# Macaron block in float32: values ahead of the correction in the speculated units, and a ninth half of expert weights loaded early

## The chip, the cores and the metric

The kernel runs on one core of one Trainium2 chip. The metric is the device time of one execution in microseconds. A profile of one execution gives, for each engine, what it did and what it waited for: PE (TensorE; its weight loads are listed as PEld), DVE (VectorE), ACT (ScalarE), POOL (GpSimd) and SP (SyncE, which here only issues transfers). "Lnnn" is a line of the kernel.

## The reference

The input is 8 batches of 1024 tokens of width 512, all float32. Three residual steps follow each other: half of a mixture-of-experts layer, an attention, and half of the same mixture-of-experts layer again.

```python
x = x + 0.5 * ffn(layernorm(x))
x = x + attention(layernorm(x))
x = x + 0.5 * ffn(layernorm(x))

def ffn(x):                                # 32 experts, each takes 8 tokens of each batch
    probs = softmax(x @ gate_w.T + gate_b, axis=tokens)
    vals, idx = top_k(probs, 8)            # over the tokens, for each expert
    merged = sum_k vals * x[idx]           # one row for each expert and batch
    h = gelu([merged, 1] @ w1)             # w1: 32 x 513 x 2048
    o = [h, 1] @ w2                        # w2: 32 x 2049 x 512
    return scatter_add(zeros, idx, vals * o)

def attention(x):                          # 16 heads of 32, causal linear attention
    q, k, v = exp(x @ Wq.T + bq), exp(x @ Wk.T + bk), x @ Wv.T + bv
    num = q . cumsum(k v^T);  den = q . cumsum(k)
    return (num / den) @ Wo.T + bo
```

## The kernel before

**Stages.** First the gate of the first expert layer for all batches, then the first 32 experts (`experts(0, ...)`), then the attention batch by batch, then the experts again (`experts(1, ...)`) and a last pass that adds their outputs to the chosen tokens. The expert weights come from memory in halves of 2 MB (`load_half`), four for each expert: two of `w1`, two of `w2`. `place` gives the tile for half number n; eight tiles are used in turn. In the last experts these are tiles of the attention's own memory (`xt0` to `xt2`, `un0`, `un1`), two of a pool `big1`, and one, `c9`, in memory of the spilled units. `preload` loads halves 0 to 3 while the attention still runs.

**Attention.** A batch has 8 chunks of 128 tokens, numbered c, and 4 units of two chunks, numbered u. For batches 0 to 3 a unit's projections to q, k and v are made in the attention (`project`). For batches 4 to 7 (`NB0 = 4`) they were made from the input alone while the first experts waited for weights (`speculate`) and were spilled to memory in `ahead_d`. When the attention comes to such a unit (`project_rest`), the spilled values (`pre`, 1.5 MB for a unit) are read back and corrected for what the first expert layer added to x. `project_rest` is a generator with four steps:

1. scales: one over the deviation spread over the partitions (L641, L649), `pmr` on POOL (L651), `pre` scaled on POOL (L655), and the next unit's `pre` requested (L713)
2. the correction of q and k: matmuls L667 into the PSUM tiles `sp0` and `sp1`, sums on DVE (L676) into `un`, exponentials on ACT (L679)
3. the values: matmuls L687, sums on DVE (L697) into `va`
4. running sums of the keys on DVE (L720) and the product `qk` on POOL (L731)

A chunk then takes: `scores` (L777, into `sp0` and `sp1`; masked on DVE at L788 for one half, copied by ACT at L793 and masked by POOL at L795 for the other), at even c the `denominators` (L739, reciprocal at L747) and their spreading (L758, L765), `turn_keys` (L827, L829), `project_out` of the chunk before (L891, L898 and its moments), and `attend` (numerators L841 and L853, product with the denominators L862, key-value sums L873).

**Around a chunk.** `begin(b + 1)` scatters the first experts' outputs into the next batch's tokens (`scatter_two`, L293, L300, L308, with moments at L314). `route(b - 1)` is the gate of the second expert layer for the batch before: logits scaled (`gate_scale`), the 8 largest of each expert chosen (`choose`: top 8 at L408, their replacement at L413, their indices at L415, softmax at L417 and L420), the chosen weights transposed (L523), merged rows (L543), and their transposes (L566). All three are generators that the loop in `attention` advances with `next`, once or more in a chunk.

**What sets the order.** The order in the program is a scheduler's, which starts from the order in which the loop issues the steps and moves instructions of an engine's queue by its own estimates. On the chip each engine takes its queue in that order. PSUM tiles named `ps_...` mostly share one tag `mm` with three banks; `sp0` and `sp1` have one bank pair each and serve the scores, the correction and the spreading of denominators.

**The seam to the last experts.** After the attention, 32 indirect transfers (L1557, L1558) issued by POOL gather the chosen tokens and weights into `xg` and `pg`. `prepare`, called in the middle of the experts, turns `pg`. The experts' loop issues `first(e)` (w1, L1233) and `second(e - 1)` (w2, L1256) as their halves arrive.

Of the kernel before, what the change touches and what calls it, by code (L numbers as in the profile page):

```python
# [15 lines left out]
P = 128  # L16
# [4 lines left out]
def kernel(  # L21
# [382 lines left out]
    def choose(t, lg, rows, g, name, listed=False, el=None):  # L404


        top = t.p2.tile([P, 8], F32, tag="top", name=f"top_{name}")
        nc.vector.max(top[rows, :], lg[rows, :])  # L408
        pinned = el is not None
        sm = t.p2.tile([P, 3], F32, tag="sm", name=f"sm_{name}")  # L410
        nc.vector.tensor_scalar_mul(sm[rows, 0:1], top[rows, 0:1], -1.0)
        rest = pm[:, g, :]
        nc.vector.match_replace(rest[rows, :], top[rows, :], lg[rows, :], -1.0e30)  # L413
        if listed and not pinned:
            nc.vector.max_index(chosen_idx[rows, g, :], top[rows, :], lg[rows, :])  # L415
        el = el if pinned else lg
# [6 lines left out]
        if pinned:  # L423
            tc.keep_in_program_order(kept)
        nc.vector.reciprocal(sm[rows, 2:3], sm[rows, 1:2])
        if pinned:
            return rest, sm[rows, 2:3], top
        return rest, sm[rows, 2:3]
# [51 lines left out]
    def route(t, s, b, el=None):  # L480
# [28 lines left out]
        chosen, r, *top = choose(t, lg, rows, g, f"b{b}", True, el)  # L509
# [113 lines left out]
    def project_rest(t, s, b, u):  # L623
# [35 lines left out]

        qkT = open_unit(t, s, b, u)  # L660
# [21 lines left out]
        yield  # L682

        ps = [t.mm.tile([P, D], F32, tag="mm", name=f"ps_v_{b}_{u * U + i}") for i in range(U)]
        for i in range(U):
            r = slice(E * ((b + i) % 4), E * ((b + i) % 4 + 1))
            nc.tensor.matmul(  # L687
                ps[i],
                lhsT=pmr[r, i * P : (i + 1) * P],
                rhs=s["oWv", i][r, :],  # L690
                start=True,
                stop=True,
            )
        for i in range(U):
            c = u * U + i
            va = t.a2.tile([P, D], F32, tag="va", bufs=3, name=f"va_{b}_{c}")
            nc.vector.scalar_tensor_tensor(  # L697
                va,
                pre[:, (2 * NDC + i * 2) * UT : (2 * NDC + i * 2 + 2) * UT],
                rs[:, c : c + 1],  # L700
                ps[i],
                ALU.mult,
                ALU.add,
            )
            s["va", b, c] = va
# [244 lines left out]
    def attention(t, early, preload):  # L950
# [46 lines left out]
        last = None  # L997
        for b in range(B):
            for c in range(NCH):
# [23 lines left out]
                if b == B - 1 and c == NCH - 2:  # L1023
                    late.close()
                    preload(1)
                    preload(2)
                    preload(3)
                    el = end.enter_context(tc.tile_pool(name="el", bufs=1, side="right")).tile(
                        [P, S], F32, name="el"
                    )  # L1030
                    gate = route(t, s, b, el)
                if rest and c % U:
                    turn_keys(t, s, b, c)
                    next(ahead)
                    next(gate, None)
                scores(t, s, b, c)
# [28 lines left out]
                if last is not None:  # L1065
                    project_out(t, s, *last)
                    if c == 0:
                        for h in range(2):
                            store_x(out, s["xt", b - 1][0], b - 1, h)
                        gate_sums(t, s, b - 1, range(NCH // 2, NCH))  # L1070
                        gate = route(t, s, b - 1)
                    if c == NCH // 2:
                        gate_sums(t, s, b, range(c))
                    if b == B - 1 and c == NCH - 2:
                        gate_sums(t, s, b, range(NCH // 2, c))
                    if b == B - 1 and c == NCH // 2:
                        store_x(out, s["xt", b][0], b, 0)
                if c % U == 0:
                    spread_denominators(t, s, b, c // U)
                else:  # L1080
                    if rest and c > 1:
                        next(begun, None)
                    next(ahead, None)
# [5 lines left out]
                if rest and c % U == 0:  # L1089
                    next(ahead)  # L1090
# [101 lines left out]
    def experts(f, place, loaded, beside=iter(()), aside=None):  # L1192

        with ExitStack() as stack:
            hp = stack.enter_context(tc.tile_pool(name=f"hp{f}", bufs=2))
# [99 lines left out]
            for e in range(E + 2):  # L1295
# [12 lines left out]
                if e == E // 2 and aside is not None:  # L1308
                    aside()
# [212 lines left out]
    keep, loaded, pools = ExitStack(), {}, {}  # L1522

    def place(n, shape, name):
        k = n % 8
# [17 lines left out]
    with ExitStack() as stack:  # L1543
# [3 lines left out]
        tk = stack.enter_context(tc.tile_pool(name="tk", bufs=1))  # L1547
        out_rows = out.rearrange("b s d -> (b s) d")
        pmT_rows = pmT_d.rearrange("b s e -> (b s) e")


        xg = tk.tile([P, 2, K, D], F32, name="xg")
        pg = tk.tile([P, 2, K, E], F32, name="pg")
        for g in range(2):
            for k in range(K):
                at = bass.IndirectOffsetOnAxis(ap=chosen_idx[:, g, k : k + 1], axis=0)
                nc.gpsimd.indirect_dma_start(pg[:, g, k, :], None, pmT_rows, at)  # L1557
                nc.gpsimd.indirect_dma_start(xg[:, g, k, :], None, out_rows, at)  # L1558
        pgT = tk.tile([P, 2, K, E], F32, name="pgT")
        to = tk.tile([P, 2 * K], U32, name="to")  # L1560

        def prepare():


            for g in range(2):
# [103 lines left out]
```

## Time and profile before

| what | value |
| --- | --- |
| time, median of 3 runs | 2604.76 us (2601.95 to 2608.11) |
| the profiled execution's own time | 2606.22 us |
| its span, first to last instruction | 2604.5 us |
| mean granted TensorE clock | 0.915 |
| PE busy | 2190.8 us (84%) |
| DVE busy | 862.3 us (33%) |
| ACT busy | 500.4 us (19%) |
| POOL busy | 376.6 us (14%) |
| halves of expert weights | 256, of 2048 KB |

The span has four stages: the first gate to about 120 us, the first experts to about 812 us, the attention to about 1960 us, and the last experts to the end. In the profile's rows of 40 slices a digit is a share in tenths; a slice lasts 65.1 us. "PEclk" is the clock that TensorE was granted, as a share of full speed. In an answer by stretches of time, the columns after the stretch are its length, the busy time of each engine with the number of its instructions, the granted clock, the share of the time in which the 16 DMA engines were busy, and GB/s. In a timeline a row is a start, a duration, the engine, line and operation, what it writes and reads, a count, and in brackets how long the engine sat idle before it and whom it waited for.

### The profile page before, as it was taken

What the parts mean: (1) busy time and instruction counts of PE and PEld (TensorE: products, weight loads), DVE (VectorE), ACT (ScalarE), POOL (GpSimd) and SP (SyncE); (2) the same over time, 40 slices, a digit from 0 to 9 for tenths busy, and PEclk for the clock granted to TensorE, in tenths of its full rate; (3) what the DMA queues carried; (4) which work ended last, traced back from release to release, by engine and by line L of the source; (5) the groups of instructions that cost most, each with busy time, mean ns of one, the idle gap of its engine ahead of it and who ended that gap; (6) DMA issues with size and microseconds to landing.
All of it is one profiled execution on the core that took longest, in us unless ns stands there. A gap on an engine that the chain in (4) does not pass through costs nothing.

```text
span 2604.5 us, 41783 instructions
## 1 busy us (share of the span) xinstructions
PE 2190.8 (84%) x18679; PEld 1153.6 (44%) x18679; DVE 862.3 (33%) x1495; ACT 500.4 (19%) x965; POOL 376.6 (14%) x345
## 2 busy tenths in 40 slices
PE   8799999898986999999999989999986565555555
PEld 5354545444533666666666655555551111101111
DVE  6411111111102443444534466777750000100002
ACT  6310000000000322222223243343430000000000
POOL 0000000000000212111122145545324000000002
PEclk9999999999998999999999989989888878777788
DMA  7799999999996000010100233333159999999995
GB/s 276 305 426 427 427 427 427 426 427 428 427 429 255 1 18 1 21 50 20 52 9 19 79 110 124 106 113 109 68 210 389 425 427 428 428 428 428 428 427 239
DMA packets 95635, 668.22 MB, mean 257 GB/s; under 512 B 18254, under 2 KB 22606, under 8 KB 58592
## 3 DMA queue, kind: packets, MB, share of 16 engines
q1 hardware_dynamic: 73952, 621.71, 58.1%
q10 hardware_dynamic: 18432, 35.66, 3.5%
q0 software_dynamic: 3072, 8.19, 0.8%
q8 instruction: 146, 2.39, 0.4%
q14 instruction: 33, 0.27, 0.0%
HBM read 614.34 MB, written 48.23 MB: 254 GB/s over the span
## 4 chain that ended last, share of the span: by engine, by line
PE 50%; issue 23%; DMA 16%; DVE 5%; ACT 2%; POOL 1%; SPq 0%; POOLq 0%; ACTq 0%; DVEq 0%
DMA w<-in_w 11%; PE ps_o L891 8%; PE ps_k L603 4%; PE ps_q L603 4%; PE ps_v L811 4%; PE ps_sk L1143 3%; PE ps_sq L1143 3%; PE p_ps L1256 3%; PE h_ps L1233 3%; PE ps_n L841 2%; PE sp L777 2%; PE ps_n L853 2%; PE ps_sv L1160 2%; DMA xg<-out,chosen_idx 2%; PE ps_sc L293 1%
## 5 line engine op out<-in xcount | busy, mean ns | idle before, releaser
L1233 PE MATMUL h_ps<-w,mT 128*8 128x512 f32 x2048 | 294.4, 703 | 126.2 <-DMA w<-in_w 124.3
L1242 DVE STREAM_TRANSPOSE hs<-h_ps 128x512 f32<-128x512 f32 x64 | 45.9, 717 | 721.6 <-PE h_ps L1233 716.3
L1256 PE MATMUL p_ps<-w,pm 128*32 128x512 f32 x1024 | 168.9, 790 | 130.3 <-DMA w<-in_w 122.0
L891 PE MATMUL ps_o<-wo_sb,at 128*128 128x512 f32 x512 | 258.5, 652 | 0.2
L1233 PEld LDWEIGHTS h_ps<-w,mT 128*8 128x8 f32 x2048 | 51.2, 95 | 342.4 <-issue 208.7
L1256 PE MATMUL p_ps<-w,gl 128*32 128x512 f32 x1024 | 133.5, 654 | 38.6 <-DMA w<-in_w 38.3
L594 POOL TENSOR_TENSOR xt<-xt,bo_sb 128x512 f32<-128x512 f32 x32 | 45.8, 1447 | 763.1 <-PE ps_ocT L338 703.4
L1256 PEld LDWEIGHTS p_ps<-w,pm 128*32 128x32 f32 x1024 | 36.0, 127 | 265.7 <-issue 136.5
L891 PEld LDWEIGHTS ps_o<-wo_sb,at 128*128 128x128 f32 x512 | 102.0, 210 | 115.0 <-issue 110.0
L795 POOL TENSOR_SCALAR_AFFINE_SELECT am<-am 128x512 f32<-128x512 f32 x128 | 79.0, 642 | 398.7 <-ACT am L793 260.8
L314 DVE BATCH_NORM_STATS2 st<-xt 128x6 f32<-128x512 f32 x192 | 128.4, 684 | 5.1 <-DMA xt<-in_x 2.5
L603 PE MATMUL ps_k<-xnT,wk_sb 128*128 128x256 f32 x512 | 115.3, 383 | 10.8 <-ACT xnT L339 10.8
L1249 ACT ACTIVATE pm<-a 128x128 f32<-128x128 f32 x32 | 9.9, 309 | 586.5 <-DVE a L1244 580.5
L1143 PE MATMUL ps_sq<-xcT,wq_sb 128*128 128x256 f32 x512 | 118.7, 388 | 4.1 <-ACT xcT L241 4.1
L1143 PE MATMUL ps_sk<-xcT,wk_sb 128*128 128x256 f32 x512 | 117.4, 385 | 0.0
L1160 PE MATMUL ps_sv<-wv_sb,xcT 128*128 128x512 f32 x256 | 115.6, 599 | 0.0
L811 PE MATMUL ps_v<-wv_sb,xnT 128*128 128x512 f32 x256 | 115.1, 593 | 0.0
L603 PE MATMUL ps_q<-xnT,wq_sb 128*128 128x256 f32 x512 | 115.1, 382 | 0.0
L1143 PEld LDWEIGHTS ps_sq<-xcT,wq_sb 128*128 128x128 f32 x512 | 96.8, 193 | 35.3 <-issue 17.4
L1143 PEld LDWEIGHTS ps_sk<-xcT,wk_sb 128*128 128x128 f32 x512 | 96.8, 192 | 27.6 <-issue 15.0
L603 PEld LDWEIGHTS ps_k<-xnT,wk_sb 128*128 128x128 f32 x512 | 95.8, 190 | 28.6 <-ACT xnT L339 14.7
L777 PE MATMUL sp<-un 32*128 32x128 f32 x2048 | 104.8, 302 | 3.9 <-DVE un L676 3.8
(246 smaller groups left out, 2846.3 us busy)
## 6 DMA issues: line engine op xcount, KB each, us to landing
w<-in_w SPq DMA_DIRECT2D x256, 2048.0 KB, 29.8
xt<-in_x SPq DMA_DIRECT2D x31, 1024.0 KB, 10.8
pre<-ahead_d SPq DMA_DIRECT2D x16, 1536.0 KB, 6.5
ahead_d<-ahead_qk ACTq DMA_DIRECT2D x16, 1024.0 KB, 11.5
out<-xt SPq DMA_DIRECT2D x16, 1024.0 KB, 5.4
xs<-in_x ACTq DMA_DIRECT2D x16, 512.0 KB, 19.7
ahead_d<-ahead_v ACTq DMA_DIRECT2D x16, 512.0 KB, 11.0
pm<-pm SPq DMA_DIRECT2D x16, 128.0 KB, 2.5
```

What stands on the lines that cost most here:

```text
L314: nc.vector.bn_stats(st, xt[:, c, :])
L603: nc.tensor.matmul(ps[:, o, :], lhsT=w_sb[n][:, dc, oc * P : (oc + 1) * P], rhs=xnT[:, dc, :], start=(dc == 0), stop=(dc == NDC - 1),)
L777: nc.tensor.matmul(sp[r // 2][:, r % 2, og, :], lhsT=kT[hr, og, cols], rhs=qT[hr, og, cols], start=True, stop=True,)
L795: nc.gpsimd.affine_select(out=am[1][:, i, :, :], in_=am[1][:, i, :, :], pattern=[[0, NDC], [1, P]], compare_op=ALU.is_ge, fill=0.0, base=0 ...
L811: nc.tensor.matmul(ps, lhsT=s["xnT", b, c // U][:, dc, cols], rhs=w_sb["v"][:, dc, :], start=(dc == 0), stop=(dc == NDC - 1),)
L841: nc.tensor.matmul(ps[hr, og, :], lhsT=va[:, (og * HG + r) * HD : (og * HG + r + 1) * HD], rhs=am[r // 2][:, r % 2, og, :], start=(og == 0 ...
L853: nc.tensor.matmul(ps[hr, og, :], lhsT=kv[hr, og, :], rhs=qT[hr, og, cols], start=False, stop=True, skip_group_check=True,)
L891: nc.tensor.matmul(ps, lhsT=at[:, oc, :], rhs=w_sb["o"][:, oc, :], start=(oc == 0), stop=(oc == NDC - 1),)
L1143: nc.tensor.matmul(ps[:, o, :], lhsT=w_sb[w][:, dc, oc * P : (oc + 1) * P], rhs=xcT[:, dc, :], start=(dc == 0), stop=(dc == NDC - 1),)
L1160: nc.tensor.matmul(ps, lhsT=xcT[:, dc, i * P : (i + 1) * P], rhs=w_sb["v"][:, dc, :], start=(dc == 0), stop=(dc == NDC - 1),)
L1233: nc.tensor.matmul(h[32 * j : 32 * j + B, :], lhsT=mT[:, dc, e, :], rhs=w1h[dc // 2][:, dc % 2, j * 512 : (j + 1) * 512], start=(dc == 0), ...
L1256: nc.tensor.matmul(pp[32 * j : 32 * (j + 1), :], lhsT=gl4[e % 4][:, q, :, :].rearrange("p i b -> p (i b)"), rhs=w2h[q // (NU // 2)][:, q % ...
```

## The change

1. In `project_rest` the values (step 3) come ahead of the correction (step 2).
2. The loop in `attention` advances the generators at other places. For batches 4 to 7 the work that ends a chunk's predecessor (`project_out`, stores, gate sums, a new `route`) is put into `finish_chunk` and, at chunk 0, called ahead of the scores, followed by the running sums of the keys. At even chunks up to c = 4, after `attend`, the next chunk's keys are turned and two steps of the unit are issued. At c = 7 the values come after the scores and the correction follows the projection.
3. `choose` becomes a generator, `choosing`: the indices of the top 8 are taken before their replacement, and there is a step between. `route` has so one step more, and each later step comes one chunk later.
4. `preload(4)` loads a ninth half into a tile of its own, `d9`, in memory of the spilled units; the other eight are used in turn as before, shifted by one.
5. The gathers are issued after the second turn of the experts' loop, once `d9` has been used, and their tiles take its memory.

```diff
@@ choose
+        *_, made = choosing(t, lg, rows, g, name, listed, el)
+        return made
+
+    def choosing(t, lg, rows, g, name, listed, el=None):
...
+        in_place = el is None
+        if listed and in_place:
+            nc.vector.max_index(chosen_idx[rows, g, :], top[rows, :], lg[rows, :])
+            yield None
         nc.vector.match_replace(rest[rows, :], top[rows, :], lg[rows, :], -1.0e30)
-        if listed and not pinned:
-            nc.vector.max_index(chosen_idx[rows, g, :], top[rows, :], lg[rows, :])
...
@@ project_rest: the block of the values, unchanged in itself, goes from
   behind the exponentials to ahead of open_unit
@@ attention
+        def finish_chunk(b, c):
+            nonlocal gate
+            project_out(t, s, *last)
+            if c == 0:
+                for h in range(2):
+                    store_x(out, s["xt", b - 1][0], b - 1, h)
+                gate_sums(t, s, b - 1, range(NCH // 2, NCH))
+                gate = route(t, s, b - 1)
...
                     preload(3)
+                    pools["d"] = single.enter_context(
+                        tc.tile_pool(name="d9", bufs=1, side="right", reuse_waits="tile")
+                    )
+                    preload(4)
...
+                    for _ in gate:
+                        pass
                     gate = route(t, s, b, el)
-                if rest and c % U:
-                    turn_keys(t, s, b, c)
+                if c == 0 and b >= NB0:
+                    finish_chunk(b, c)
                     next(ahead)
+                if rest and c % U and c < NCH - 1:
                     next(gate, None)
+                    if c > 1:
+                        next(begun, None)
                 scores(t, s, b, c)
...
-                if last is not None:
-                    project_out(t, s, *last)
...
+                if rest and c == NCH - 1:
+                    next(ahead)
+                if last is not None and not (c == 0 and b >= NB0):
+                    finish_chunk(b, c)
                 if c % U == 0:
                     spread_denominators(t, s, b, c // U)
                 else:
-                    if rest and c > 1:
-                        next(begun, None)
                     next(ahead, None)
...
                 attend(t, s, b, c)
-                if rest and c % U == 0:
+                if rest and c % U == 0 and c < NCH - 2:
+                    turn_keys(t, s, b, c + 1)
+                    next(ahead)
                     next(ahead)
@@ place
-        k = n % 8
+        if n == 4:
+            return pools["d"].tile(shape, F32, name=name)
+        k = n % 8 if n < 4 else (n - 1) % 8
@@ last experts
+        def gather():
+            single.close()
+            tk = stack.enter_context(tc.tile_pool(name="tk", bufs=1, reuse_waits="tile"))
...
-        experts(1, place, loaded, aside=prepare)
+        experts(1, place, loaded, asides={1: gather, E // 2: prepare}, outer=stack)
```

In the changed file the lines of the steps are L670 and L680 (values), L698, L707 and L710 (correction), L727 and L738 (running sums and `qk`), L784, L795, L800 and L802 (scores and their masks), L848 and L860 (numerators), L869 (product with the denominators), L898 (projection), L530, L550 and L573 (the gate's products) and L1214 (weights).

## The prediction, made before the run

> **What bounds it.** I read the page first, then windows by stage, then PE's waits and timeline in the stage that the diff touches.
>
> ```profile
> PE 2190.8 (84%) x18679; PEld 1153.6 (44%) x18679; DVE 862.3 (33%) x1495; ACT 500.4 (19%) x965; POOL 376.6 (14%) x345
> ...
> PEclk9999999999998999999999989989888878777788
> DMA  7799999999996000010100233333159999999995
> ```
>
> Slices are 65 us. The last experts (from slice 30) are bound by weights, the attention (slices 12 to 29) by PE. The diff touches the attention of batches 4 to 7 (1494 to 1930) and the seam to the experts. Batch 5 there, cut where PE starts or ends a named step:
>
> ```profile
> core 0: us, PE busy (x) PEld busy (x) DVE busy (x) ACT busy (x) POOL busy (x), PEclk, DMA share, GB/s
> 1634.16:1659.31 25.15, 23.16 (x332) 13.62 (x328) 22.90 (x37) 12.29 (x23) 10.72 (x10) 0.93 0.22 82
> 1659.31:1678.56 19.25, 17.95 (x227) 12.15 (x217) 13.57 (x23) 5.69 (x13) 7.30 (x6) 0.82 0.28 91
> 1678.56:1690.06 11.50, 11.50 (x187) 6.30 (x185) 8.52 (x15) 3.05 (x5) 9.64 (x8) 1.00 0.44 129
> 1690.06:1716.96 26.90, 25.00 (x342) 15.39 (x333) 17.46 (x28) 9.83 (x19) 12.56 (x10) 0.87 0.40 142
> 1610.90:1634.16 23.26, 21.79 (x304) 12.30 (x294) 14.79 (x21) 10.90 (x21) 10.06 (x8) 0.93 0.28 101
> ```
>
> These are stretch B (chunks 1, 2), C (chunk 3), D (chunk 4), E (chunks 5, 6) and A (chunk 7 of batch 4 with chunk 0 of batch 5): 106.06 us. PE seems busy, but the clock falls in B, C, E and A, and DVE is busy 22.9 of 25.15 us in B. Windows of 3.41 us show the falls:
>
> ```profile
> 1612.55:1615.96 3.41, 2.25 (x35) 0.99 0.00 0
> 1615.96:1619.37 3.41, 3.41 (x5) 0.51 0.70 234
> 1636.40:1639.80 3.40, 2.10 (x41) 1.00 0.02 7
> 1639.80:1643.20 3.40, 3.40 (x5) 0.50 0.87 314
> ```
>
> A window in which PE idles 1.2 to 1.3 us is followed by one at half clock, which costs 1.7 us of work. Chunk 5 in full:
>
> ```profile
> 1690.06 1.15 PE L667 MATMUL ps_qk<-pmr,oW 32*128 32x256 f32 x16
> 1691.14 0.66 PE L827 MATMUL ps_kt<-ident,un 128*128 128x128 f32 x4
> 1691.72 1.13 PE L687 MATMUL ps_v<-oWv,pmr 32*128 32x512 f32 x4
> ...
> 1694.36 1.89 PE L566 MATMUL ps_mT<-isum,m 128*128 128x32 f32 x8 [1.30 <-DVE va L697]
> ...
> 1704.38 1.08 PE L841 MATMUL ps_n<-am,va 128*32 128x128 f32 x32
> ```
> ```profile
> 1696.51 2.65 DVE L720 TENSOR_TENSOR_SCAN un<-ones,un,un 128x256 f32<-128x256 f32 x4
> ...
> 1699.33 2.35 POOL L731 TENSOR_TENSOR qk<-un 128x1024 f32<-128x1024 f32 x1 [10.94 <-DVE un L720]
> 1701.63 1.23 POOL L795 TENSOR_SCALAR_AFFINE_SELECT am<-am 128x512 f32<-128x512 f32 x2
> ```
>
> The gate's matmul waits 1.30 for a PSUM bank that DVE frees only after the correction's sums. But also see the chain scans, key product, causal select, numerators: it ends at 1702.9, covered because PE comes at 1704.4.
>
> **The change, by its steps.** PE at full clock, start to start in this trace: output projection 3.63, scores 1.11, the two numerator groups 1.01 each, key-value sum 0.38, correction 1.0, key turn 0.59, one value 0.45, scatter pair 1.06. I walk each stretch in the order in which the built program of the changed kernel queues its instructions.
>
> The correction (L698, sums L707, exponentials L710) goes behind the values (L670, L680); no instruction is added or dropped, only queued elsewhere.
>
> E (batches 4 to 6). Turn 0.6, values to 1.45, correction to 2.45, the gate's L543 product (1.74, now here) to 4.2, scatters to 5.25; DVE has read the correction by 4.9, so the scores run to 6.35 without the 1.30 wait. The projection needs the bank of the first scatter, read at 7.75: it runs 7.85 to 11.5. DVE after the correction: the four scans (0.67 each) now have among them the moments and centring of the merged rows (1.6), two scatter sums (0.66 each), their two statistics (0.69) and aggregates (0.15), and the mask product (1.20): 8.4 us, so the last scan ends at 13.3 (before: 9.0). On POOL the key product L731 stands ahead of the select: 13.3+2.35+1.23 = 16.9. PE idles from 11.5 to 16.9. Then 0.8+1.01+0.38+1.11+1.7 (denominators, scale, turn)+3.63+0.64+0.9 (mT, moved here)+2.4 brings it to 29.55. After such a gap 3.4 to 5.6 us run at half clock: 2.5 more. 32.0 against 26.9: **+5.1**.
>
> C. Correction to 2.45, a scatter pair (moved ahead) to 3.5, scores wait to 5.0 for DVE's read and end at 6.0, projection 9.6. Scatter sums and statistics put the mask product at 10.2, and two bias adds (1.25 each), now ahead of the select on POOL, put the select at 10.6. Numerators, sums, scatters and scores end at 14.95, plus 0.7 of half clock not hidden: 15.65 against 19.25, **-3.6** (2.0 of it is the gate's transposing product L523, moved to D).
>
> D. The same with L523 (2.0) for L543 (1.74): **+0.25**.
>
> B. The values' two DVE instructions (0.70 each) now precede the correction's sums, so exponentials, gate copies (2.1), score copy (0.99) and select start 1.2 later: numerators wait to 11.9. DVE then has the top-8 steps before the reciprocal, which ends at 22.4. End 25.55, plus 0.45 of half clock: 26.0 against 25.15, **+0.9**.
>
> A. Scores 1.1, values 2.0, projection 5.6, correction 6.65, numerators 8.67. The next projection, now directly behind, needs DVE's product, queued behind the correction's sums (to 9.6): starts 10.4, so a new wait of 1.7, with half clock after it (1.7). End 22.9 against 23.26: **-0.3**.
>
> So B to E give +2.65 and A -0.3. Batch 4 enters worse: there three scans stand ahead of the product and five scores ahead of the projection (+2.3 instead of -0.3), although its first scores run inside a POOL wait of 6.6. Batch 7 has no next batch to scatter: A -0.3, B +1.5, C -3.5, E +1.1 = -1.2. Sum: (2.3+2.65)+2.35+2.35-1.2 = +8.45. The same adding for before gives 104 per batch (86.7 work, 7 waits, 10 lost to the clock) where the trace has 106, so four batches get +1 each: **+12.5**.
>
> **The rule on clocks.** [...] I sum by the trace.
>
> **Ninth half.** One more half (2.1 MB) is queued before the experts:
>
> ```profile
> 1925.00:1930.00 5.00, 5.00 (x58) 1.00 0.01 3
> 1930.00:1935.00 5.00, 4.43 (x79) 1.00 0.00 0
> ...
> 2300.00:2500.00 200.00, 115.69 (x664) 21.10 (x664) 11.48 (x22) 3.40 (x11) 0.00 (x0) 0.79 1.01 428
> ```
>
> From 1922 to 1934 the DMA moves nothing while SP waits for the unit tile `un1`; the new half fits in, behind `un0`'s load at 1914.6. At 428 GB/s it is worth 2.097/428 = 4.9 us, and PE (58% busy) follows. The gathers move behind the second expert's use of that memory: 32 issues on POOL (about 60 us) that nothing needs before expert 16. Before, the first of them filled a DMA gap at 1957 to 1965 that now stays partly empty: +0.5. If the memory came free late, SP would hold the store and the next four halves behind it; bounds -4.9 and +5, taken **-4.4**, since the last reader of the spilled units is done by about 1905.
>
> **At nothing.** The split of `choosing` adds no instruction; in batches 1 to 3 the gate's PE steps come one chunk later, beside PE at 98% and clock 1.00, which hides DVE's shift (uncovered: 1.2 us per batch; bounds -2 and +3). Input loads behind `pre` on SP have a chunk of slack. At chunk 0 `finish_chunk` now issues two stores and the gate's sums before the scores instead of after: on SP they precede only loads that are wanted two chunks later; on PE the projection then no longer covers the reciprocal behind the scores (0.5 and 0.3 of wait, inside A's 22.9). The key turn of an odd chunk goes ahead of the values, its copy (0.59) ahead of the exponentials on ACT; inside B, C and E. The route of batch 6 is drained at chunk 6 of batch 7: its last step (0.9) moves there from chunk 5, beside full PE work. Total: 12.5-4.4 = **+8**. The profiled execution took 2606.22 (span 2604.5), 1.5 above the median; I put the 8 on the median: 2612.8.
>
> **Rivals.** (1) Faster: the new waits do not trip the clock. Place: the waits of 1.7 (A), 1.2 (B), 1.4 (C). It decides at the idle time per window: 0.5 did not trip, 1.16 did; split over two windows they stay under. With E's also spared, a batch takes 103.0 against 106.06, in all -10-4.4: 2590. For it: each is one wait in place of two losses. Against: E's gap is 5 us wherever the windows fall. (2) No change: half of these windows trip and my +4 is not needed: 2600 to 2610. (3) The ninth half does not come early, as SP is held: 2617; the idle DMA speaks against it.
>
> **Numbers.** 0.2% (5.2 us) is about what a measurement can tell from no change. Slower by E's chain 0.47 (rival 3 in it), no change 0.28, faster 0.25. Range 2594 to 2624: -15 takes in most of rival 1, +19 two more microseconds per batch and half the late-memory bound.
>
> **What would show it.** After: in chunk 5 of batches 4 to 6 numerators (L848) waiting about 5 us for POOL's select, and POOL for the scan L727; no wait on the value sums at L388, L530, L573; a wait of 1.7 before the first projection of a batch; DMA busy at 1922 to 1934 and 4.9 us less from the first experts' matmul to the end. If chunk 5's gap is under 2 us, or the clock stays at 1.0 in B and C, the forecast is wrong on the fast side.

## The result, and the profile after

| | before | after |
|---|---|---|
| time, median (range), us | 2606.19 (2601.95 to 2608.11) | 2622.81 (2622.11 to 2625.65) |
| ratio to before, 95% interval | | 1.0067 [1.0054, 1.0080] |
| span of the profiled execution | 2604.5 | 2621.0 |
| entry of batch 4 (end of PE's key-value sum of batch 3, chunk 6) | 1497.92 | 1498.84 |
| the same point in batch 7 | 1922.41 | 1942.01 |
| first matmul of the last experts | 1960.75 | 1981.27 |
| from there to the end | 643.73 | 639.78 |

The medians are of six executions each; the three of the first section are among those of before. The change makes the kernel 16.6 us slower: slower, as forecast, but by twice the 8 us. The forecast's 2612.8 us is 10 us too low; the measured time lies inside its range, 1.2 us below the upper end. In the profiled executions the loss is 0.9 us ahead of batch 4, 18.7 in batches 4 to 7 and 0.9 between their last chunk and the experts; 4.0 come back in the experts. The page of after, for the three lines of before that the forecast began with:

```profile
PE 2187.8 (83%) x18679; PEld 1152.5 (44%) x18679; DVE 881.7 (34%) x1495; ACT 501.8 (19%) x965; POOL 383.0 (15%) x345
...
PEclk9899999999988999999999999998997778777777
DMA  7799999999995000010010323233159999999995
```

The page looks much the same. DVE has the same 1495 instructions and 19.4 us more busy time, so some of them have become longer: by the trace the gate's 8 index adds (L541) take 7.2 us more in all, its 8 scaled diagonals (L518) 6.7 and the 96 scans of the keys (L727) 6.2. That was the first hint at what the forecast had missed. The stretches of batch 5, in the order A, B, C, D, E:

```profile
core 0: us, PE busy (x) PEld busy (x) DVE busy (x) ACT busy (x) POOL busy (x), PEclk, DMA share, GB/s
1619.97:1640.97 21.00, 19.11 (x303) 11.17 (x294) 14.71 (x21) 10.43 (x19) 6.92 (x7) 1.00 0.34 126
1640.97:1668.37 27.40, 24.57 (x335) 14.83 (x328) 24.27 (x34) 13.11 (x25) 15.10 (x12) 0.94 0.18 64
1668.37:1684.92 16.55, 15.65 (x210) 9.47 (x200) 15.72 (x24) 5.31 (x12) 8.46 (x6) 0.90 0.26 97
1684.92:1696.39 11.47, 11.47 (x186) 7.72 (x185) 7.31 (x13) 3.42 (x6) 9.05 (x7) 1.00 0.44 129
1696.39:1729.04 32.65, 26.66 (x357) 15.66 (x348) 19.57 (x31) 9.94 (x19) 12.93 (x10) 0.90 0.35 121
```

E is 32.65 us, forecast 32.0. The clock is better than before in four of five rows; what grew is PE's idle time. Over batches 4 to 7 (the same windows by batch) PE is busy 391.9 us before and 389.0 after, and idle 32.6 and 54.2. Where PE waits, before from 1494 to 1930 and below it after from 1500 to 1950 (what waits, for whom, us in total, how often, the longest):

```profile
PE ps_rs L388 <- DVE va L697: 5.2, 4, 1.3
PE ps_pmT L523 <- DVE va L697: 5.2, 4, 1.3
PE ps_mT L566 <- DVE va L697: 5.2, 4, 1.3
...
PE ps_n L841 <- POOL am L795: 1.5, 8, 0.2
```
```profile
PE ps_n L848 <- POOL am L802: 18.6, 11, 3.3
PE sp L784 <- DVE un L707: 6.3, 13, 0.7
PE ps_v L670 <- POOL pmr L658: 5.3, 1, 5.3
PE ps_o L898 <- DVE at L869: 4.9, 4, 1.5
PE ps_o L898 <- DVE xt L308: 4.2, 3, 1.4
PE ps_n L848 <- DVE am L795: 3.9, 4, 1.2
PE ps_v L670 <- DVE xt L905: 3.6, 2, 1.8
```

The three waits for the value sums (15.6 us before) are gone, as the change says. The wait of 5.3 at the entry of batch 4 was there before too (6.6). In place of the three stand waits for POOL's causal select (1.5 before; of the 18.6 some 10 are in chunk 5 of batches 4 to 6 and 6.4 at the end of chunk 1), for DVE's product (L869) and scatter sum (L308), and 3.6 us of value products (L670) that wait for the residual add L905, in two batches only. All four batches, cut at the end of each chunk's key-value sum, change in us (forecast ahead of the slash; its +1 a batch is not spread):

| | A | B | C | D | E | sum |
|---|---|---|---|---|---|---|
| batch 4 | +2.3 / -0.4 | +0.9 / +1.4 | -3.6 / **+1.6** | +0.25 / 0.0 | +5.1 / +5.6 | +4.95 / +8.1 |
| batch 5 | -0.3 / -0.9 | +0.9 / +0.9 | -3.6 / -2.7 | +0.25 / 0.0 | +5.1 / +5.8 | +2.35 / +3.0 |
| batch 6 | -0.3 / -0.9 | +0.9 / +0.6 | -3.6 / **+2.5** | +0.25 / +1.3 | +5.1 / +5.0 | +2.35 / +8.4 |
| batch 7 | -0.3 / -0.9 | +1.5 / +0.6 | C and D: -3.5 / -2.4 | | +1.1 / +1.7 | -1.2 / -0.9 |

The miss stands in two cells, chunk 3 of batches 4 and 6. They are 11.2 us above the forecast, while all four batches are 10.2 above it (18.7 against 8.45), so the other cells together came out 1.0 below. The rest of the section shows first the chain that was forecast, then those two cells.

**Chunk 5, as forecast.** PE and POOL in batch 5:

```profile
1696.39 0.65 PE L834 MATMUL ps_kt<-ident,un 128*128 128x128 f32 x4
...
1704.41 3.70 PE L898 MATMUL ps_o<-wo_sb,at 128*128 128x512 f32 x8 [1.39 <-DVE xt L308]
1709.34 0.41 PE L848 MATMUL ps_n<-am,va 128*32 128x128 f32 x4 [1.23 <-DVE am L795]
1713.10 2.50 PE L848 MATMUL ps_n<-am,va 128*32 128x128 f32 x28 [3.35 <-POOL am L802]
```
```profile
1706.29 2.87 POOL L643 TENSOR_TENSOR xt<-xt,bo_sb 128x512 f32<-128x512 f32 x2 [11.56 <-DVE st L314]
1710.12 2.34 POOL L738 TENSOR_TENSOR qk<-un 128x1024 f32<-128x1024 f32 x1 [0.95 <-DVE rs L989]
1712.41 1.22 POOL L802 TENSOR_SCALAR_AFFINE_SELECT am<-am 128x512 f32<-128x512 f32 x2
```

POOL's key product starts 13.7 us after the chunk's start (forecast 13.3), and the numerators behind its select 16.7 us after it (forecast 16.9). PE stands still for 1.39, 1.23 and 3.35 us, then runs at half clock (2.50 for 28 products; 1.08 for 32 in chunks at full clock). The half clock lasts 6.8 us, where the forecast's estimate was 3.4 to 5.6:

```profile
1712.31:1719.14 6.83, 6.04 (x112) 4.56 (x116) 0.69 (x1) 0.27 (x1) 1.32 (x3) 0.50 0.10 37
```

**Chunk 3, not forecast.** DVE at the end of chunk 2 in batch 5 and, below, in batch 6:

```profile
1665.22 0.20 DVE L541 TENSOR_SCALAR chosen_idx<-chosen_idx 32x8 uint32<-32x8 uint32 x1
1665.34 2.41 DVE L518 TENSOR_SCALAR diag<-ident,sm_b 32x32 f32<-32x32 f32 x1
...
1774.91 2.24 DVE L541 TENSOR_SCALAR chosen_idx<-chosen_idx 32x8 uint32<-32x8 uint32 x1
1777.07 2.40 DVE L518 TENSOR_SCALAR diag<-ident,sm_b 32x32 f32<-32x32 f32 x1
1779.49 0.69 DVE L905 TENSOR_TENSOR xt<-ps_o,xt 128x512 f32<-128x512 f32 x1
```
```profile
1665.37 4.67 POOL L662 TENSOR_TENSOR pre<-pre,rsb 128x1024 f32<-128x1024 f32 x2
...
1774.77 4.66 POOL L662 TENSOR_TENSOR pre<-pre,rsb 128x1024 f32<-128x1024 f32 x2
```
```profile
1780.33 2.66 PE L670 MATMUL ps_v<-oWv,pmr 32*128 32x512 f32 x3 [1.77 <-DVE xt L905]
```

Two steps on 32x8 and 32x32 numbers take 2.24 and 2.40 us. POOL's scaling of `pre` is two multiplies of 2.35 us: in batch 6 they end at 1777.12 and 1779.43, and the two DVE steps end at 1777.15 and 1779.47. In batch 4 the same (2.24 and 2.40, beside a multiply that starts at 1553.40). In batch 5 DVE comes to the index add 0.15 us ahead of the multiply, it takes 0.20, and only the diagonal is held. The residual add behind them starts 1.5 us after the end of chunk 2 in batches 4 and 6, and 0.8 us ahead of it in batch 5. It frees a PSUM bank; the values wait 1.78 and 1.77 us for that, and half clock follows, 6.8 and 10.2 us of it. In before, the diagonal took 0.30 to 0.63 us in these batches and the index add 0.17: they ran earlier, away from this multiply. What brings them beside it is the new order of values and correction: with the swap alone (experiment 10) the index add takes 2.25 and 2.24 us in batches 4 and 6 and the diagonal 2.40 and 2.41 in batches 4 to 6, so the split of `choosing` is not needed for it. Why a step beside a multiply is held until that ends, no run shows.

### The profile page after: what moved, and what is told of

Read it like the earlier page. It is cut to its first block, busy times and chain, and to the rows that moved or that the text cites. A ratio compares the mean times of both kernels' runs of the same rounds, so it can differ in the third digit from the quotient of the medians.

```text
span 2621.0 us, 41808 instructions
## 1 busy us (share of the span) xinstructions
PE 2187.8 (83%) x18679; PEld 1152.5 (44%) x18679; DVE 881.7 (34%) x1495; ACT 501.8 (19%) x965; POOL 383.0 (15%) x345
## 4 chain that ended last, share of the span: by engine, by line
PE 49%; issue 22%; DMA 16%; DVE 6%; POOL 2%; ACT 2%; POOLq 0%; ACTq 0%; DVEq 0%; SPq 0%
DMA w<-in_w 11%; PE ps_o L898 7%; PE ps_k L610 4%; PE ps_q L610 4%; PE ps_v L818 4%; PE ps_sq L1168 3%; PE ps_sk L1168 3%; PE h_ps L1258 3%; PE p_ps L1281 3%; PE ps_n L848 3%; PE sp L784 2%; PE ps_n L860 2%; DMA pg<-pmT_d,chosen_idx 2%; PE ps_sv L1185 2%; DVE un L707 1%
## 5 line engine op out<-in xcount | busy, mean ns | idle before, releaser
L1258 PE MATMUL h_ps<-w,mT 128*8 128x512 f32 x2048 | 280.6, 681 | 115.9 <-DMA w<-in_w 115.4
L1281 PE MATMUL p_ps<-w,pm 128*32 128x512 f32 x1024 | 182.7, 851 | 135.6 <-DMA w<-in_w 129.0
L898 PE MATMUL ps_o<-wo_sb,at 128*128 128x512 f32 x512 | 241.5, 614 | 9.8 <-DVE at L869 4.9
L898 PEld LDWEIGHTS ps_o<-wo_sb,at 128*128 128x128 f32 x512 | 94.5, 195 | 115.2 <-issue 100.3
L802 POOL TENSOR_SCALAR_AFFINE_SELECT am<-am 128x512 f32<-128x512 f32 x128 | 79.9, 648 | 426.6 <-ACT am L800 282.3
L610 PEld LDWEIGHTS ps_k<-xnT,wk_sb 128*128 128x128 f32 x512 | 95.8, 190 | 28.4 <-ACT xnT L339 14.6
L1168 PEld LDWEIGHTS ps_sk<-xcT,wk_sb 128*128 128x128 f32 x512 | 96.0, 190 | 26.8 <-issue 14.5
L784 PE MATMUL sp<-un 32*128 32x128 f32 x2048 | 99.7, 294 | 8.2 <-DVE un L707 6.3
## 6 DMA issues: line engine op xcount, KB each, us to landing
xs<-in_x ACTq DMA_DIRECT2D x16, 512.0 KB, 18.4
```

The lines of the kernel that those rows point to most:

```text
L610: nc.tensor.matmul(ps[:, o, :], lhsT=w_sb[n][:, dc, oc * P : (oc + 1) * P], rhs=xnT[:, dc, :], start=(dc == 0), stop=(dc == NDC - 1),)
L784: nc.tensor.matmul(sp[r // 2][:, r % 2, og, :], lhsT=kT[hr, og, cols], rhs=qT[hr, og, cols], start=True, stop=True,)
L802: nc.gpsimd.affine_select(out=am[1][:, i, :, :], in_=am[1][:, i, :, :], pattern=[[0, NDC], [1, P]], compare_op=ALU.is_ge, fill=0.0, base=0 ...
L898: nc.tensor.matmul(ps, lhsT=at[:, oc, :], rhs=w_sb["o"][:, oc, :], start=(oc == 0), stop=(oc == NDC - 1),)
L1168: nc.tensor.matmul(ps[:, o, :], lhsT=w_sb[w][:, dc, oc * P : (oc + 1) * P], rhs=xcT[:, dc, :], start=(dc == 0), stop=(dc == NDC - 1),)
L1258: nc.tensor.matmul(h[32 * j : 32 * j + B, :], lhsT=mT[:, dc, e, :], rhs=w1h[dc // 2][:, dc % 2, j * 512 : (j + 1) * 512], start=(dc == 0), ...
```

## The experiments

Each ratio is to the kernel before, run on the same chip; after is 1.0067. A difference of 0.001 is 2.6 us.

**1. Scatters of the odd chunks back behind the projection** (this undoes what makes chunk 5's chain long):

```diff
                 if rest and c % U and c < NCH - 1:
                     next(gate, None)
-                    if c > 1:
-                        next(begun, None)
...
                 else:
+                    if rest and 1 < c < NCH - 1:
+                        next(begun, None)
                     next(ahead, None)
```

> The changed kernel with one move undone: at odd chunks of batches 4 to 6 the scatter pair of the next batch is queued behind the output projection again, not ahead of the scores. Theory (chain of chunk 5): the scans stand directly behind the correction again, GpSimd's key product and select end about 5 us earlier, the gap of 3.35 us ahead of the numerators falls below 1, and with its half clock chunk 5 goes from 21.4 to about 17 us in three batches; chunk 3 gives back up to 2 us in each. Net 7 to 12 us faster than the changed kernel, 2611 to 2616. Rival (the values ahead of the correction are what makes the scans late): the gap stays at 2 to 3 us, chunk 3 loses what it had gained, 2621 to 2628.

Measured: 2612.91 us, 1.0023 [1.0014, 1.0032], 11 us off the changed kernel: the theory. Its 22 executions reach from 2605.18 to 2620.64, and the profiled one is the fastest, so its chunks gain more than 11 us. POOL and PE in chunk 5 of batch 5, which starts at 1690.60 here:

```profile
1700.10 2.35 POOL L738 TENSOR_TENSOR qk<-un 128x1024 f32<-128x1024 f32 x1 [12.76 <-DVE un L727]
```
```profile
1703.09 0.41 PE L848 MATMUL ps_n<-am,va 128*32 128x128 f32 x2 [0.83 <-POOL am L802]
```

The key product starts 9.5 us into the chunk instead of 13.7, and the wait of 3.35 becomes 0.83 (0.18 more behind it). In this execution chunk 5 goes from 21.6, 21.6 and 21.3 us in batches 4 to 6 to 15.5, 17.1 and 15.5. Chunk 3 gave nothing back (17.7, 14.5, 17.5 against 17.5, 14.6, 18.4), so the moved scatters were never what shortened it in batch 5.

**2. The ninth half taken out of the changed kernel, 3. put alone into the kernel before:**

```diff
-                    pools["d"] = single.enter_context(
-                        tc.tile_pool(name="d9", bufs=1, side="right", reuse_waits="tile")
-                    )
-                    preload(4)
```

with `place`, the gathers and `asides` of the old or the new form to match.

> The changed kernel without the ninth half (its load, the memory map and the place of the gathers as before). Theory: the ninth half is worth 4.0 us between the first matmul of the experts and the end; all of the loss is in the attention. So 4 us slower than the changed kernel, 2626 to 2627. Rival (its load disturbs the last chunks through SyncE's queue or the DMA, so that part of the 0.9 us lost between the last chunk and the experts comes from it): 2.5 to 3 us slower only; or no difference, if the shorter stage comes from the later start alone.

> The kernel before with the ninth half alone (load, memory map, gathers behind the second expert), its steps in the old order. Theory: the halves add independently, 4 us faster than before, about 2602. Rival (in the old order the experts begin 20 us earlier and the DMA is already the limit, the gathers fill a gap that the new half only takes from them): within 1 us of before, 2605 to 2607.

Measured: without it 2629.32, 1.0084 [1.0071, 1.0097], 4.4 us slower than the changed kernel, as the theory has it; alone in the kernel before 2607.05, 0.9994 [0.9984, 1.0003], a gain of 1.6 us that could also be none: the rival's side. From the experts' first matmul to the end: 645.1 without and 642.3 with, in the profiled executions. DMA had moved 18.3 MB in the 75 us ahead of that matmul in the changed kernel, 17.9 with the half alone, 15.7 before, so the half came early in both. Why it brings less in the kernel before was not found. Over all the kernels of this document this stretch takes 643.5 to 645.1 us in the four without the half and 638.2 to 642.3 in the ten with it.

**4. Both small steps of the gate taken away from POOL's multiply:**

```diff
+            tc.keep_in_program_order(
+                nc.vector.tensor_scalar_add(
+                    chosen_idx[rows, g, :], chosen_idx[rows, g, :], float(int(name[1:]) * S)
+                )
+            )
             yield None
...
-        scaled = nc.vector.tensor_scalar_mul(diag[rows, :], ident[rows, rows], r)
+        if el is None:
+            scaled = nc.scalar.activation(
+                diag[rows, :], ident[rows, rows], AF.Copy, scale=r
+            )
+        else:
+            scaled = nc.vector.tensor_scalar_mul(diag[rows, :], ident[rows, rows], r)
...
-        nc.vector.tensor_scalar_add(chosen_idx[rows, g, :], chosen_idx[rows, g, :], float(b * S))
+        if el is not None:
+            nc.vector.tensor_scalar_add(
+                chosen_idx[rows, g, :], chosen_idx[rows, g, :], float(b * S)
+            )
```

`el is None` holds for the gates of all batches but the last.

> The changed kernel with the two small steps of the gate taken off the stretch of VectorE that runs beside GpSimd's bias multiply: the 32x8 index add directly behind the index search, the 32x32 scaled diagonal on ScalarE. [...] Without them the wait of 1.77 and the half clock behind it go, batches 4 and 6 look like batch 5 in chunk 3: 2.9 and 3.8 us less there and 1.2 in chunk 4 of batch 6, so 6 to 8 us faster than the changed kernel, 2615 to 2617 us. Rival (VectorE is simply full there, the long durations are an artefact of the record): the residual add comes 0.5 us earlier at most, 0 to 1 us faster, 2622.

Measured: 2631.88, 1.0100 [1.0085, 1.0115]: a miss, 9 us slower. Chunk 3 did what was expected of it (14.3 us in batches 4 and 6), but the pinned index add pushed the gate's replace step to later (41.4 us after the end of the last key-value sum of batch 5, against 35.9 in the changed kernel), and with it ScalarE's work. PE waited 2.29 us for ScalarE's `rsb` in chunk 2 of batch 6 (20.7 us against 15.8). The edit moved more than it was meant to.

**5. The diagonal alone on ScalarE:** the part of that diff on `scaled`. By the author's estimate it keeps what experiment 4 gained in chunk 3, without its loss: 4 to 7 us off the changed kernel.

> The changed kernel with one instruction of the gate per batch on another engine: the 32x32 scaled diagonal on ScalarE instead of VectorE, all else queued as it was. In the run with both small steps moved, chunk 3 became 3.2 and 4.1 us shorter in batches 4 and 6 (profiled executions), but a pinned index add pushed the gate's replace step back and with it ScalarE's copies, so chunk 2 grew by as much. [...] Rival (the time comes back as waits and half clock elsewhere, as in that run): 2621 to 2626.

Measured: 2629.61, 1.0098 [1.0083, 1.0112]: again a miss in the time, and again right in place: chunk 3 took 14.3 and 14.6 us in batches 4 and 6, and batch 6 as a whole 109.3 (113.9). But batch 4 was entered 5.0 us later and took 5.0 us longer; its chunk 2 fell into half clock for four windows (shown in the last section). The gates of batches 0 to 2, which run in batches 1 to 3, had their diagonal on ScalarE too, and that is where the late entry comes from. ScalarE and PE in batch 2:

```profile
1246.56 0.32 ACT L519 ACTIVATE diag<-ident,sm_b 32x32 f32<-32x32 f32 x1 [3.63 <-DVE sm_b L431]
1246.91 0.84 ACT L624 ACTIVATE un<-ps_k,bk_sb 128x256 f32<-128x256 f32 x2
```
```profile
1247.80 1.55 PE L903 MATMUL ps_o<-wo_sb,at 128*128 128x512 f32 x3 [1.84 <-ACT un L624]
```

ScalarE stands still for 3.63 us until DVE has the reciprocal that scales the diagonal, and two exponentials of the keys stand behind it in its queue. The projection waits for them, 4.2 us over the three batches; the changed kernel has no such wait.

**6. The diagonal on ScalarE only for the gates of batches 3 to 6:**

```diff
-        scaled = nc.vector.tensor_scalar_mul(diag[rows, :], ident[rows, rows], r)
+        if 3 <= b < B - 1:
+            scaled = nc.scalar.activation(
+                diag[rows, :], ident[rows, rows], AF.Copy, scale=r
+            )
+        else:
+            scaled = nc.vector.tensor_scalar_mul(diag[rows, :], ident[rows, rows], r)
```

> The changed kernel with the scaled diagonal on ScalarE only for the gates that run inside batches 4 to 7 (those of batches 3 to 6); in the earlier run it stood on ScalarE in all of them, and batch 4 then began 5 us later and lost another 8 us at its chunks 0 and 2 to half clock, with the same waits as before. Theory: the 5 us ahead of batch 4 go, chunk 3 keeps its 3 to 4 us in batches 4 and 6: 2615 to 2618, 5 to 8 us faster than the changed kernel. Rival (the half clock at chunk 2 of batch 4 follows from the diagonal itself): 2622 to 2626.

Measured: 2612.85, 1.0029 [1.0021, 1.0037], 10 us off the changed kernel by one 32x32 instruction in four places. DVE in chunk 2 of batch 6 (the index add is L546 here, the residual add L910):

```profile
1773.67 2.25 DVE L546 TENSOR_SCALAR chosen_idx<-chosen_idx 32x8 uint32<-32x8 uint32 x1
1775.96 0.69 DVE L910 TENSOR_TENSOR xt<-ps_o,xt 128x512 f32<-128x512 f32 x1
```
```profile
1777.25 1.68 PE L675 MATMUL ps_v<-oWv,pmr 32*128 32x512 f32 x3
```

The index add is still held to the end of a multiply, the residual add follows at once, and the values have no wait. Chunk 3 took 14.9, 14.3 and 14.6 us in batches 4 to 6, 6.7 less in all. Batch 4 is entered at 1499.14, and PE's waits for L624 ahead of it are gone. The profiled execution is 4.7 us slower than the median and loses some of the gain again, 3.9 us of it in the first stretch of batch 4.

**7, 8. Both repairs together**, with the diagonal on ScalarE for all gates, and for those of batches 3 to 6: the diffs of 1 and 5, and of 1 and 6.

> The changed kernel with the scatter pair of odd chunks back behind the projection (worth 10 us by itself) and the scaled diagonal on ScalarE. Theory: the two losses lie in different chunks (5 and 3) and add: 14 to 17 us faster than the changed kernel, 2606 to 2609. Rival (with the scatters back, chunk 3 has other waits and the diagonal no longer decides): 2612 to 2614, as with the scatters alone.

> The changed kernel with the scatter pair of odd chunks back behind the projection and the scaled diagonal on ScalarE only for the gates of batches 3 to 6. With it for all gates batch 4 began 8 us later than without. Theory: those 8 us go, the rest stays: 2597 to 2600, 4 to 7 us faster than the kernel before. Rival (the late entry was a matter of that one execution, and the two causes overlap): 2604 to 2607, no difference from the kernel before.

Measured: 2605.35, 1.0007 [0.9996, 1.0017], and 2595.95, 0.9962 [0.9949, 0.9976]. The two losses lie in different chunks, and repairing one does not take away the gain of the other: 27 us off the changed kernel for the second pair, more than the 11 and 10 of its parts. It is 10 us faster than before. With them the four batches take 420.7 us in the profile, before 424.5, changed 443.2.

**9. The projection at chunk 0 behind the scores again:**

```diff
                 if c == 0 and b >= NB0:
-                    finish_chunk(b, c)
                     next(ahead)
...
-                if last is not None and not (c == 0 and b >= NB0):
+                if last is not None:
                     finish_chunk(b, c)
```

> The changed kernel with the output projection of chunk 7 (and the stores and gate sums that go with it) behind the scores of chunk 0 again in batches 4 to 7, the scans still ahead. Theory: that move took 0.9 us off the chunk 0 stretch in each of three batches (21.0 against 21.9) and hides the wait for the product; undoing it costs 0 to 4 us, 2623 to 2627. Rival (the early projection is what sends VectorE into the later chunks behind time): 4 to 8 us faster, 2615 to 2619.

Measured: 2644.35, 1.0148 [1.0134, 1.0161], 21 us slower: neither side of the expectation had the size. A goes from 21.0 to 24.6 us in batch 5: with the scans queued at chunk 0 and no projection ahead of them, PE waits 2.23 us for the exponentials (L710) and 2.32 for the key product (L738). So the early projection is cover for the late scans. Compared with the order before (21.9), the two moves together bring only 0.9.

**10. The swap alone,** in the kernel before: the values' step and the correction's change places in `project_rest`, nothing else.

```diff
         yield
+        ps = [t.mm.tile(...)]          # values, L687 and L697 of before
+        ...
+        yield
         qkT = open_unit(t, s, b, u)    # correction
         ...
         yield
-        ps = [t.mm.tile(...)]
-        ...
-        yield
         sum_keys(t, s, b, u)
```

> The kernel before with the one swap that names the change: in a unit of batches 4 to 7 the values' step ahead of the correction's, each in the other's old place; scatters, gate, chunk 0 and weights as before. Theory: the swap does what it is for, the three waits of 1.3 us a batch on the value sums (15.6 us in all over four batches) go, VectorE's 1.4 us of value sums stand ahead of the correction's and take some back: 3 to 8 us faster than before, 2599 to 2604. Rival (the scores now wait for the correction's sums instead, and the exponentials, scans and the key product behind them come a chunk later, as in chunk 5 of the changed kernel): 3 to 12 us slower, 2610 to 2619.

Measured: 2612.86, 1.0030 [1.0018, 1.0041], the rival's side. But its executions reach from 2597.87 to 2623.0, 25 us, where those of the kernel before beside it span 11; the fastest has the mean clock 0.926, the slowest 0.914. Six of the 22 lie at 2603 or below and the other 16 at 2610.9 or above. The profiled one, at 2601.84, is of the six; what the others do differently no trace shows. It has no wait on the value sums left, chunk 5 at 14.2 us (16.7 before) and chunk 3 at 18.0, 15.6 and 17.9: its index add and diagonal stand beside the multiply here too.

**11, 12. The swap with the diagonal on ScalarE for the gates of batches 3 to 6, with and without the ninth half.**

> The kernel before with the three parts that have gained something or might: the swap of values and correction in the old places, the ninth half, and the scaled diagonal of the gates of batches 3 to 6 on ScalarE. The swap alone took 2612.9 us, with its fastest execution at 2597.9. Theory: the diagonal held the residual add in chunk 2 here too (2.41 us), so 2 to 5 us off the swap, and 3 off by the ninth half: 2604 to 2608. Rival (the swap's slow executions come from the clock alone and nothing else moves them): 2609 to 2611.

> The best kernel so far but for the ninth half: the kernel before with the swap of values and correction and the scaled diagonal of the gates of batches 3 to 6 on ScalarE, weights and gathers as before. Theory: the ninth half is worth some 3 us (in the profiled executions the stretch from the experts' first matmul to the end is 638 to 642 us with it, 644 to 645 without), so 2599 to 2600 here against 2596 with it. Rival (the timed difference of the ninth half alone, none that could be measured, is the right one): 2595 to 2597.

Measured: 2596.19, 0.9959 [0.9945, 0.9972], better than either side of the expectation, and 2599.48, 0.9975 [0.9966, 0.9984]. The first beats both kernels, and equals experiment 8 within its interval. Their difference, 0.0016 or 4.2 us, is the ninth half (3.8 in the profiles: 639.8 and 643.6 us behind the first matmul of the experts); the two intervals overlap. Against the swap alone the diagonal is worth 14 us between the medians, but the profiled executions take 418.8 and 419.4 us in batches 4 to 7, since that of the swap alone is one of the six.

## Why the prediction was right or wrong

**Right: the sign, and the mechanism of E.** The chain of scans, key product, select and numerators came out within 0.5 us, and the first experiment shows that the moved scatters, and with them this chain, cost 11 us in all. It could be worked out because each duration stood in the trace of before and only the order was new. The values' waits went, and D stayed near nothing in batches 4 and 5 (+1.3 in batch 6).

**Right: the ninth half.** -4.4 forecast; 4.4 and 4.2 timed as a difference (each uncertain by about as much), 4.0 between the two profiles, though 1.6 or nothing in the kernel before. The forecast's rival 3, that the half does not come early, falls.

**Wrong: the size, in the term C (chunk 3).** -3.6 in each of batches 4 to 6; measured +1.6, -2.7, +2.5. Two steps failed. C was read from batch 5 of before, where chunk 3 takes 17.3 us; in batches 4 and 6 it takes 15.9, one half-clock window less, so 1.4 of the 3.6 was never to be had there. And DVE's queue was added up with each small step at its duration of before: the index add and the diagonal were counted as next to nothing (0.17 and 0.3 to 0.6 us), but in their new place they take up to 4.6 us. With the diagonal away (experiment 6) chunk 3 changes by -1.0, -3.0 and -1.3 us, so that C, with the 1.4 taken off, is still 0.6 to 1.2 us too good. Every held step shown above ends within 0.05 us of the end of a multiply (in batch 6 at 1777.15 and 1779.47, the multiplies at 1777.12 and 1779.43). With the durations of the new place (2.24 and 2.40 us, in batch 5 0.20 and 2.41) DVE would have been later by an estimated 1.8 to 4.2 us at the end of chunk 2 in batches 4 to 6; moving the diagonal away (experiment 6) is worth 10 us. The row that should have led there was in before's trace, a diagonal of 0.63 us in batches 5 and 7 beside 0.30 in batches 4 and 6:

```profile
1652.79 0.63 DVE L511 TENSOR_SCALAR diag<-ident,sm_b 32x32 f32<-32x32 f32 x1
```

It ends at 1653.42, and one of POOL's two bias adds, which began at 1652.12, ends at 1653.39.

**Wrong: A in batch 4, and the half clock in A.** +2.3 forecast, -0.4 measured in batch 4; elsewhere the wait of 1.7 came (1.49), but the clock stayed at 1.00 behind it, so A fell by 0.9 instead of 0.3.

**The +1 a batch** (4 in all) was an allowance without a mechanism, and no run shows one. It brought the total nearer by luck; A's better result used up most of it. Costed at nothing and not so: 0.9 us ahead of batch 4, and 0.9 between the last chunk and the experts.

**The rule on the clock.** The forecast took from the trace of before that an idle of 1.2 us in a window halves the next. The changed kernel (1.49 us and no fall) and experiment 10 (0.07 us and a fall) speak against that, as the last section shows.

## What to carry to other kernels

When an order changes, do not carry durations over: look for each VectorE step at what GpSimd runs beside it in the new place, however small the step is (here an add on 32x8 numbers went from 0.17 to 2.24 us). Before a stretch of one repetition is taken for all, compare it in every repetition; two of three differed here. A named gain (waits of 15.6 us, all removed) is not a time: the chain that now ends last, and the clock, took it back. A step given to an idle engine takes its wait along and holds what is queued behind it there (experiment 5: 3.63 us).

## What the runs showed of the hardware

**VectorE beside GpSimd.** Besides the two steps above, the index add of experiment 6 is held to 1775.92, and the first of the two multiplies beside it ends at about 1775.9 (they take 4.68 us together). ScalarE's diagonal beside the same multiply takes 0.32 us:

```profile
1773.55 4.68 POOL L667 TENSOR_TENSOR pre<-pre,rsb 128x1024 f32<-128x1024 f32 x2
```
```profile
1773.78 0.32 ACT L519 ACTIVATE diag<-ident,sm_b 32x32 f32<-32x32 f32 x1 [4.16 <-DVE sm_b L431]
```

DVE's larger steps take longer beside POOL's too, and POOL's beside DVE's. In the changed kernel two scans in chunk 3 of batches 4 to 6 take 1.30 and 1.61 us beside POOL's bias adds (L643), where 0.73 is the median, and a bias add takes 1.65 us beside them and 2.25 beside the gate's L426, where 1.27 is the median. In the kernel before, scans of 1.66 to 1.78 us and bias adds of 2.28 to 2.30 stand beside each other in batches 1 to 3. With the scatters moved back (experiment 1) chunk 3 hardly changes, and with the diagonal alone moved (experiment 6) it gets its time back, so the scans are not what it lost by.

**Idle time alone does not decide the clock.** In batches 4 to 7 of the two kernels each stretch of half clock lasts one to four times 3.41 us (3.41, 6.83, 10.24 or 13.65), so the windows here have that length. In the kernel before the forecast's rule fits all windows that lie in batches 4 to 6: half clock begins behind 0.9 to 1.3 us of idle time, and never behind 0.6 or less. It does not fit the others. The changed kernel, around the wait of 1.49 us in A, and below it the swap alone (experiment 10) at chunk 3 of batch 6, windows of 3.41 us:

```profile
1626.98:1630.39 3.41, 1.92 (x61) 1.46 (x54) 3.38 (x6) 1.71 (x4) 0.00 (x0) 1.00 0.02 5
1630.39:1633.80 3.41, 3.41 (x8) 1.25 (x8) 2.11 (x4) 2.99 (x6) 1.15 (x1) 1.00 0.89 314
```
```profile
1769.97:1773.38 3.41, 3.34 (x50) 3.12 (x44) 3.06 (x4) 1.81 (x5) 0.00 (x0) 1.00 0.02 5
1773.38:1776.80 3.42, 3.42 (x17) 1.73 (x10) 3.32 (x5) 2.76 (x6) 1.04 (x1) 0.50 0.85 287
```

PE is idle for 1.49 us and the clock stays; PE is busy for 3.34 of 3.41 us and the next window is at half clock. The window ahead of the fall holds only products over 32 rows:

```profile
1770.04 1.75 PE L523 MATMUL ps_pmT<-diag,pm 32*128 32x32 f32 x15
...
1771.74 2.48 PE L777 MATMUL sp<-un 32*128 32x128 f32 x31
```

In experiment 10 the three windows of batches 4 to 6 ahead of a fall idle 0.07 to 0.19 us, and windows with up to 1.53 us have none behind them. Counting work instead of time was tried: the moving columns of each window (instructions times columns) weighted by contraction rows over 128. Windows ahead of a fall then have 815 to 1382 in the kernel before and 1020 to 1034 in experiment 10; those ahead of none 2207 and more, and 1589 and more. In the changed kernel it fails: falls come behind windows of up to 3664, and windows from 1724 up have none behind them. What decides a fall stays open; no run was made for it.

**A fall can last.** Chunk 2 of batch 4 in experiment 5:

```profile
1547.57:1550.98 3.41, 1.63 (x40) 0.99 (x40) 2.72 (x6) 2.08 (x4) 2.86 (x3) 1.00 0.55 215
1550.98:1554.39 3.41, 3.41 (x39) 1.75 (x41) 3.35 (x6) 0.00 (x0) 0.00 (x0) 0.50 0.04 11
1554.39:1557.81 3.42, 3.42 (x44) 2.35 (x37) 0.80 (x2) 1.23 (x2) 0.00 (x0) 0.50 0.00 0
1557.81:1561.22 3.41, 3.41 (x34) 2.38 (x33) 3.27 (x5) 1.01 (x1) 1.93 (x2) 0.50 0.00 0
1561.22:1564.63 3.41, 3.41 (x10) 2.18 (x10) 3.38 (x4) 0.96 (x2) 3.41 (x5) 0.50 0.00 0
```

Four windows at half clock though PE is busy throughout. At half clock the same products take longer (28 numerators 2.50 us in chunk 5 of the changed kernel, 32 take 1.08 at full clock) and spread over more windows; whether that is what keeps the clock down was not tested. The changed kernel has the same wait at that place (1.67 us for POOL's select) and no fall; its chunk 2 takes 14.6 us, this one 19.7. In both nearly all of the wait lies in one window, with 1.64 and 1.78 us of idle time, so what makes the difference is not shown. Falls like this one may be why some of these kernels spread over 10 to 25 us from one execution to the next, and why the edits of experiments 4 and 5 cost more in one batch than they gained in the others; that link was not tested.
